# The end of a scan kernel: other planned costs, paired norms and other shares of engines behind the last scan

## The chip, the cores and the metric

The kernel runs on one core of a Trainium2 chip. The metric is the device time of one execution in microseconds (us), the median over runs. The engines are named as in the profile: PE is TensorE, PEld its weight loads, DVE is VectorE, ACT is ScalarE, POOL is GpSimd and SP the engine that here only issues transfers.

## The reference, cut to what matters

The input has 4 batches of 64 x 64 positions with 96 channels, in float32.

```
x = x + conv(group_norm(x))        # layer norm, projections, a scan over 4096 positions
t = x as [4, 4096, 96]
t = t + attn(layer_norm(t))        # linear attention: no softmax
t = t + ffn(layer_norm(t))         # 96 -> 384 -> 96, rounded to fp8 and fp16

# the scan, 96 channels x 16 states:
h = d * (A_t * h) + d * (B_t * u_t);  y = gate * sum(C_t * h)

# ffn, with q_mul to 5 exponent and 2 mantissa bits, q_acc to 5 and 10:
h = relu(q_acc(q_acc(q_mul(x) @ q_mul(W1)) + q_mul(b1)))
y = q_acc(q_acc(q_mul(h) @ q_mul(W2)) + q_mul(b2))
```

The attention has no softmax, so all keys and values of a batch shrink to one 97 x 96 matrix (called r here), and the attention of a position is a product with it. The matrix of a batch needs every position of the batch, so the attention and the feed-forward of a batch come only after its last scan.

## The kernel before, in words

A batch is cut into 8 chunks of 512 positions (`NCH`, `TC`), each held as 128 partitions x 4 rows (`J`) x 96 channels. There are 32 chunks. Each goes through 12 tiles of 128 partitions (32 channels x 4 states), so the scan stage has 384 steps (`K`). Each step does the projections on PE, the products and the scan on DVE, copies on ACT and a product on POOL. All other work is put beside these steps by a table of steps (`AT`, written by hand, through `at`): the preparation of chunks ahead (`front`), the `tail` of the chunk just scanned (state sum, gate, output projection, residual, layer norm, transposed copy, Gram matrix), `attn_matrix` once a batch, and the `ffn` of the batch before. The tile framework doesn't reorder: each engine works in the order in which the program writes its instructions.

What can't be put ahead of step 384 is left over: the last tail, the last `attn_matrix`, the feed-forward of all 8 chunks of the last batch, and parts of the feed-forward of the batch before (chunks 5, 6 and 7 of it). I write (b, i) for chunk i of batch b, counted from 0; the last batch is 3. This end is ordered by a planner (`Plan`, kept in `end`). `tail`, `attn_matrix` and `ffn` make jobs instead of table entries: an engine, a cost in us, the jobs it follows (`after`), buffers it takes and frees, and `late`, the time from the end of its instruction to the result being there. `run` schedules the jobs once by (time, rank, longest rest of the chain) and then 1500 times more with random offsets to the rank, keeps the order whose planned end is earliest, and writes the instructions in that order. The plan decides order alone; on the chip each engine waits for semaphores. Where PE is planned to be idle for over 0.8 us, `stay_awake` products are written to keep its clock up.

A layer norm (`LayerNorm`) has three steps: `stats` on DVE (`bn_stats`, `bn_aggr`), `rstd` on POOL (add eps, power -0.5, and for an apply on ACT also minus mean times root), then `apply` on ACT (four activations) or `apply_vector` on DVE (four tensor_scalar). The power works on 4 columns, one of each row of the partition.

One whole chunk in the end runs these steps: `fetch` (a transfer on SP), `attention` (PE), `residual` and `stats` (DVE), `rstd` (POOL), `apply` (ACT, or DVE where `vector` is true: chunks 0 and 4 of the last batch), `transpose` (PE), `quant_in` (ACT), three times `hidden` (PE), `round_hidden` (ACT) and `relu_vector` (DVE), then `quant` (ACT for i % 3 == 0, else POOL), `project_out` (PE), `round_out` (ACT), `bias_out` and `total` (POOL; on DVE for the last two chunks) and `store` (SP).

The lines of the profile named here: L836, L852, L845 the products and the scan of a step; L374 and L376 `stats`; L381, L395, L386 and L387 the four steps of `rstd`; L399 `apply`; L406 `apply_vector`; L900 `state_sum`; L979 `gram_sum`; L1044 to L1059 the chain to r; L1093 `fetch`; L1098 `attention`; L1103 `residual`; L1113 `transpose`; L1120 `quant_in`; L1124 `hidden`; L1141 `round_hidden`; L1145 `relu_vector`; L1150 and L1152 `quant` on ACT and POOL; L1158 `project_out`; L1165 `round_out`; L1170 `bias_out`; L1177 `total`; L1180 `store`; L1459 `stay_awake`; L620 the power of the group norm.

Of the kernel before, what the change touches and what calls it, by code (L numbers as in the profile page):

```python
# [17 lines left out]
P = 128  # L18
# [39 lines left out]
}  # L58
ON_POOL = (0, 2, 7, 8)
XBUFS = 15  # L60


@with_exitstack
def conv_attn_hybrid_kernel(
# [130 lines left out]
    mhalf = const.tile([P, J], F32, name="mhalf")  # L195
    nc.gpsimd.memset(mhalf, -0.5)

# [165 lines left out]

    class LayerNorm:


        def __init__(self, eps, nm):
            self.eps, self.nm, self.r = eps, nm, None

        def stats(self, src):  # L370
            st = small.tile([P, J, 6], F32, tag="st", name=f"st_{self.nm}")
            self.mv = small.tile([P, J, 2], F32, tag="mv", name=f"mv_{self.nm}")
            for j in range(J):
                nc.vector.bn_stats(st[:, j, :], src[:, j, :])  # L374
            for j in range(J):
                nc.vector.bn_aggr(self.mv[:, j, :], st[:, j, :])  # L376

        def rstd(self, shift=True):

            self.r = small.tile([P, J], F32, tag="rstd", name=f"rstd_{self.nm}")  # L380
            nc.gpsimd.tensor_scalar(self.r, self.mv[:, :, 1], self.eps, None, ALU.add)  # L381
            self.root()
            if not shift:
                return
            self.nmr = small.tile([P, J], F32, tag="nmr", name=f"nmr_{self.nm}")
            nc.gpsimd.tensor_scalar(self.nmr, self.mv[:, :, 0], -1.0, None, ALU.mult)  # L386
            nc.gpsimd.tensor_tensor(self.nmr, self.nmr, self.r, ALU.mult)  # L387

        def offset(self):

            self.r = small.tile([P, J], F32, tag="rstd", name=f"rstd_{self.nm}")
            nc.vector.tensor_scalar(self.r, self.mv[:, :, 1], self.eps, None, ALU.add)

        def root(self):
            nc.gpsimd.tensor_tensor(self.r, self.r, mhalf, ALU.pow)  # L395
# [19 lines left out]
    class Plan:  # L415
# [10 lines left out]
        def job(self, engine, cost, fn, *args, after=(), take=(), free=(), late=0.0):  # L426

            j = dict(
                engine=engine, cost=cost, fn=fn, args=args, take=take, free=free, late=late,
                after=[a for a in after if a], tail=None, end=None, rank=self.rank,  # L430
            )
            self.jobs.append(j)
            return j
# [5 lines left out]
        def run(self, fill=None):  # L439
# [17 lines left out]
            def schedule(bias, look):  # L457

                taken, back = {r: list(x) for r, x in self.taken.items()}, {}
                time, order = dict(self.time), []  # L460
# [3 lines left out]
                while ready:  # L464
                    best = None
                    for n in ready:
                        j = self.jobs[n]
                        t = max(time.get(j["engine"], 0.0), first[n])
                        for b in j["take"]:
                            r = b.split(":")[0]  # L470
                            if len(taken[r]) >= self.rings[r]:
                                x = taken[r][-self.rings[r]]
                                t = max(t, back[x] + self.HOP) if x in back else None
                            if t is None:
                                break
# [13 lines left out]
                    end = time[j["engine"]] = t + j["cost"]  # L489
                    for b in j["take"]:  # L490
                        taken[b.split(":")[0]].append(b)
# [44 lines left out]
    class GroupNorm:  # L536
# [82 lines left out]
        def root(self):  # L619
            nc.gpsimd.tensor_tensor(self.m[:, 1:2], self.v, mhalf[0:C, 0:1], ALU.pow)  # L620
# [60 lines left out]
    class Front:  # L681
# [3 lines left out]
        def __init__(self, b, i):  # L685
            self.b, self.i, self.nm = b, i, f"{b}_{i}"
            self.ln = LayerNorm(1e-3, f"c_{self.nm}")
            self.wd = {}
# [204 lines left out]
    def state_sum(g, last=None, first=None):  # L893
# [5 lines left out]
        for cg in range(NCG):  # L899
# [12 lines left out]
         "xs": 2, "xl": 2, "z": 2, "mv": 4},  # L912
# [16 lines left out]
    def tail(b, i):  # L929
# [68 lines left out]
        end.rank = 0  # L998
# [5 lines left out]
        if last:  # L1004
            for sh, late in ((0, 0.0), (2, 0.0), (3, 2.4)):
                w = job(f"wait{sh}", late, lambda: None)
                a = job("PE", 0.5, state_sum, g, sh, sh > 0, after=[a, w, end.last.get("o")],
                        take=["B:y"] if sh == 0 else [])
        else:
            assert state_sum in done  # L1010
        if ln.stats in done and ln.apply not in done:
            end.hold(f"mv:a{i}")
        if gated in done and project_out not in done:
            end.hold(f"yg:{i}")
        a = job("DVE", 0.7, gated, after=[a], take=[f"yg:{i}"], free=["B:y"])
        a = job("PE", 0.5, project_out, after=[a], take=[f"B:o{i}"], free=[f"yg:{i}"])
        end.last["o"] = a
        a = job("DVE", 0.56, residual, after=[a], free=[f"B:o{i}"])
        a = job("DVE", 1.1, ln.stats, t, after=[a], take=[f"mv:a{i}"])
        a = job("POOL", 1.3 if last else 1.8, ln.rstd, not last, after=[a])  # L1020
        if last:
            applied = job("DVE", 1.3, ln.apply_vector, xa, t, after=[a], free=[f"mv:a{i}"])
        else:
            applied = job("ACT", 1.55, ln.apply, xa, t, after=[a], free=[f"mv:a{i}"])
        if gram not in done:
            a = job("PE", 0.4, gram, after=[applied, end.last.get("gram")], take=[f"B:g{i}"])
            end.last["gram"] = job("DVE", 0.25, gram_sum, after=[a], free=[f"B:g{i}"])
        if transpose not in done:
            a = job("PE", 0.45, transpose, after=[applied], take=[f"C:a{i}"])
            a = job("ACT", 0.57, keep, after=[a], free=[f"C:a{i}"], take=[f"xat:{i}"])  # L1030
            end.last[b, i] = job("SP", 0.5, spill, after=[a], late=2.5, free=[f"xat:{i}"])
# [4 lines left out]
    def attn_matrix(b, s0):  # L1036
# [30 lines left out]
        end.rank, a = 0, end.last.get("gram")  # L1067
        for n, (args, out) in enumerate(chain):
# [4 lines left out]
            else:  # L1073
                a = end.job("PE", 0.3, mm, *args, after=[a], take=[f"B:r{n}"])
                a = end.last["r"] = end.job("DVE", 0.25, out, after=[a], free=[f"B:r{n}"])
# [5 lines left out]
    def ffn(b, i, s0):  # L1081
        nm = f"{b}_{i}"
        v, ln = {}, LayerNorm(1e-5, f"f_{nm}")
# [5 lines left out]
        vector = b == B - 1 and i % 4 == 0  # L1089
# [57 lines left out]
        def quant():  # L1147
            v["hq"] = sb("bu", [P, NK, TC], F8, f"hq_{nm}")
            if i % 3 == 0:
# [17 lines left out]
        def bias_out():  # L1167
            last_two = phase["end"] and b == B - 1 and i > NCH - 3
            v["yb"] = tile_of("yb", "xl", [P, J, C], F16, "yb")
            (nc.vector if last_two else nc.gpsimd).tensor_tensor(  # L1170
# [3 lines left out]
        def total():  # L1174
            v["o"] = tile_of("o", "z", [P, J, C], F32, "o")
            last_two = phase["end"] and b == B - 1 and i > NCH - 3
            (nc.vector if last_two else nc.gpsimd).tensor_tensor(v["o"], t, v["yb"], ALU.add)  # L1177
# [23 lines left out]
        end.rank = 1 + (b * NCH + i) // 4  # L1201
        if fetch in done and attention not in done:
            end.hold(f"xal:{nm}")
        if ln.stats in done and apply not in done:
            end.hold(f"mv:{nm}")
# [3 lines left out]
        def job(engine, cost, fn, *args, **kw):  # L1209
            return None if fn in done else end.job(engine, cost, fn, *args, **kw)  # L1210

        a = job("SP", 0.5, fetch, after=[end.last.get((b, i))], late=2.5, take=[f"xal:{nm}"])
        a = job("PE", 0.46, attention, after=[a, b == B - 1 and end.last["r"]], take=[f"A:a{nm}"],
                free=[f"xal:{nm}"])
        a = job("DVE", 0.57, residual, after=[a], free=[f"A:a{nm}"])
        a = job("DVE", 1.6, ln.stats, t, after=[a], take=[f"mv:{nm}"])
        a = job("POOL", 1.3 if vector else 1.8, ln.rstd, not vector, after=[a])
        a = job("DVE" if vector else "ACT", 1.9 if vector else 1.8, apply, after=[a], take=[f"xn8:{nm}"], free=[f"mv:{nm}"])
        a = job("PE", 0.45, transpose, after=[a], take=[f"C:{nm}"], free=[f"xn8:{nm}"])
        a = job("ACT", 0.6, quant_in, after=[a], take=[f"h:{nm}"], free=[f"C:{nm}"])  # L1220
        if hidden not in done:
            r, h, c = [], None, None
            for m in range(NK):
                h = job("PE", 0.24, hidden, m, after=[a, h], take=[f"M:{m}{nm}"],
                        free=[f"h:{nm}"] if m == 2 else [])
                c = job("ACT", 0.57, round_hidden, m, after=[h, c],
                        take=[f"rep:{nm}"] if m == 0 else [], free=[f"M:{m}{nm}"])
                r.append(job("DVE", 0.47, relu_vector, m, after=[c]))
            a = job(*(("ACT", 1.5) if i % 3 == 0 else ("POOL", 1.6)), quant, after=r, take=[f"bu:q{nm}"], free=[f"rep:{nm}"])
        a = job("PE", 0.5, project_out, after=[a], take=[f"A:y{nm}"], free=[f"bu:q{nm}"])  # L1230
        a = job("ACT", 0.48, round_out, after=[a],
                take=[f"xs:{nm}"], free=[f"A:y{nm}"])
        last_two = b == B - 1 and i > NCH - 3
        a = job(*(("DVE", 0.6) if last_two else ("POOL", 0.95)), bias_out, after=[a], take=[f"xl:{nm}"], free=[f"xs:{nm}"])
        a = job(*(("DVE", 0.8) if last_two else ("POOL", 0.92)), total, after=[a], take=[f"z:{nm}"], free=[f"xl:{nm}"])
        job("SP", 0.5, store, after=[a], late=2.5, free=[f"z:{nm}"])

# [159 lines left out]
    for b in range(B):  # L1397
        for i in range(NCH):
# [9 lines left out]
            first = min(24, AT["fetch"])  # L1408
# [43 lines left out]
    for s in sorted(steps):  # L1452
        if s >= K:
            call(s)
    awake = bank("D", [P, TC], "awake")
# [40 lines left out]
```

## Time and profile before

| | us |
|---|---|
| median of 3 runs | 1184.86 |
| lowest and highest run | 1181.39 and 1185.01 |
| span of the profiled execution | 1179.2 |
| the profiled execution's own time beside the span | not listed; the median stands 5.66 above the span |
| end of the last scan on DVE | 1104.26 |
| end of the last product with C on DVE | 1105.12 |
| the matrix r is copied | 1120.44 |
| end of the last total on DVE | 1173.23 |

The profile is one execution. Its page gives the busy time of each engine, 40 equal slices of the span, the chain that ended last and groups of instructions. A table of stretches gives busy times between two times, a timeline lists instructions with start and duration (neighbours of one kind merged), and the waits tell who waited for whom. The span up to about 1105 us is the scan stage, the last 74 us the end.

### The profile page before, as it was taken

Reading aid. Unit: us, or ns where it says so; the run is one execution under the profiler, and the core shown is the slowest. Engines: PE = TensorE matmul, PEld = TensorE weight load, DVE = VectorE, ACT = ScalarE, POOL = GpSimd, SP = SyncE. Lnnn points to the kernel's source line nnn. Section 1 sums busy time; section 2 is a strip of 40 time slices with the busy share of each in tenths; the row PEclk is TensorE's granted clock in tenths of the full one; section 3 lists DMA queues with packets and bytes.
Section 4 is the critical chain, followed back from the end, with each engine's and each line's share of the span. In section 5 each row is a group of like instructions: output and inputs, shape, how many; then the busy total and the mean of one; then the engine's idle time right before and its main releaser. Section 6 shows DMA issues by size and latency. Waiting matters only on the chain. (4 is left out here: it accounts for less than half of the span.)

```text
span 1179.2 us, 19184 instructions
## 1 busy us (share of the span) xinstructions
PE 1138.6 (97%) x5882; PEld 874.2 (74%) x5882; DVE 1113.3 (94%) x2079; ACT 812.9 (69%) x1833; POOL 1040.1 (88%) x1187
## 2 busy tenths in 40 slices
PE   6999999999999999999999999999999999999885
PEld 5777776777777777777777777777777777777563
DVE  6999999999999999999999999999999999999865
ACT  4666655655556777777777778777777777776475
POOL 5798888888889999999999999999999999988575
PEclk8999999999999999999999999999999999999987
DMA  7676776778876777778766776776777768766221
GB/s 184 141 165 145 169 153 156 161 163 178 177 161 148 154 162 166 163 164 191 162 160 151 170 174 159 173 165 156 156 159 159 174 155 182 159 134 146 67 65 51
DMA packets 104288, 182.12 MB, mean 154 GB/s; under 512 B 42637, under 2 KB 50769, under 8 KB 104186
## 3 DMA queue, kind: packets, MB, share of 16 engines
q1 hardware_dynamic: 90060, 106.96, 37.6%
q0 software_dynamic: 13536, 73.93, 31.4%
q8 instruction: 46, 0.75, 0.3%
q14 instruction: 56, 0.46, 0.1%
q10 hardware_dynamic: 590, 0.02, 0.0%
HBM read 69.12 MB, written 24.77 MB: 80 GB/s over the span
## 5 line engine op out<-in xcount | busy, mean ns | idle before, releaser
L836 POOL TENSOR_TENSOR bu<-bu,rep 128x512 f32<-128x512 f32 x384 | 511.9, 1343 | 42.7 <-ACT state L862 32.8
L852 DVE TENSOR_TENSOR_SCAN h<-Aps,state,bu 128x512 f32<-128x512 f32 x336 | 425.9, 1268 | 0.3 <-issue 0.2
L833 ACT ACTIVATE bu<-Bps,b_bac 128x512 f32<-128x512 f32 x384 | 262.8, 684 | 198.8 <-PE Bps L269 193.1
L845 DVE SCALAR_TENSOR_TENSOR Aps<-Aps,b_bac,rep 128x512 f32<-128x512 f32 x384 | 281.6, 733 | 4.7 <-PE Aps L269 4.3
L269 PE MATMUL Bps<-xs,w 128*128 128x512 f32 x768 | 267.1, 429 | 3.8 <-ACT bu L833 3.1
L269 PE MATMUL Aps<-xs,w 128*128 128x512 f32 x768 | 241.8, 396 | 1.2 <-DVE h L852 1.0
L885 POOL TENSOR_TENSOR ch<-ch,h 128x512 f32<-128x512 f32 x126 | 169.8, 1347 | 7.0 <-ACT ch L882 3.3
L269 PEld LDWEIGHTS Aps<-xs,w 128*128 128x128 f32 x768 | 143.9, 188 | 36.9 <-DVE h L852 2.7
L269 PEld LDWEIGHTS Bps<-xs,w 128*128 128x128 f32 x768 | 126.6, 190 | 45.8 <-ACT gx_ps L577 12.6
L269 PE MATMUL Aps<-xl,w 128*128 128x512 f32 x384 | 151.8, 395 | 0.0
L269 PE MATMUL Bps<-xl,w 128*128 128x512 f32 x384 | 151.5, 395 | 0.0
L269 PE MATMUL Dps<-xs,w 128*128 128x512 f32 x384 | 120.7, 395 | 0.0
L269 PE MATMUL Cps<-xs,w 128*128 128x512 f32 x384 | 120.6, 395 | 0.0
L876 DVE SCALAR_TENSOR_TENSOR ch<-Dps,b_bac,h 128x512 f32<-128x512 f32 x160 | 118.6, 741 | 0.4
L891 POOL DMA_DIRECT2D ch<-ch x94 | 88.9, 946 | 1.4 <-DMA ch<-ch 1.1
L269 PEld LDWEIGHTS Bps<-xl,w 128*128 128x128 f32 x384 | 72.3, 188 | 17.5
L269 PEld LDWEIGHTS Aps<-xl,w 128*128 128x128 f32 x384 | 72.1, 188 | 17.6
L269 PEld LDWEIGHTS Dps<-xs,w 128*128 128x128 f32 x384 | 72.1, 188 | 17.5
L269 PEld LDWEIGHTS Cps<-xs,w 128*128 128x128 f32 x384 | 72.1, 188 | 17.5
L882 ACT ACTIVATE ch<-Cps,b_bac 128x512 f32<-128x512 f32 x94 | 64.5, 686 | 24.2 <-PE Cps L269 24.2
L269 PE MATMUL Cps<-xl,w 128*128 128x512 f32 x192 | 75.8, 395 | 0.0
L269 PE MATMUL Dps<-xl,w 128*128 128x512 f32 x192 | 75.6, 394 | 0.0
(200 smaller groups left out, 2049.4 us busy)
## 6 DMA issues: line engine op xcount, KB each, us to landing
ch<-ch POOLq DMA_DIRECT2D x94, 768.0 KB, 6.7
rep<-ddd SPq DMA_DIRECT2D x124, 384.0 KB, 7.5
ddd<-dd SPq DMA_DIRECT2D x31, 384.0 KB, 3.2
xl<-lo SPq DMA_DIRECT2D x62, 128.0 KB, 2.4
x<-in_x_dram SPq DMA_DIRECT2D x32, 192.0 KB, 2.9
xatd<-xat SPq DMA_DIRECT2D x32, 192.0 KB, 3.6
xal<-xatd SPq DMA_DIRECT2D x32, 192.0 KB, 5.4
out_dram<-o SPq DMA_DIRECT2D x32, 192.0 KB, 2.5
```

Source lines behind the costliest of these rows:

```text
L269: nc.tensor.matmul(ps, lhsT=wt[:, n], rhs=mv, start=(n == 0), stop=(n == 2))
L833: nc.scalar.activation(self.bu, self.b_ps, AF.Identity, bias=self.bias(0))
L836: nc.gpsimd.tensor_tensor(self.bu, self.bu, rep[self.b, self.i][:, 1, self.cg], ALU.mult)
L845: nc.vector.scalar_tensor_tensor(self.a_ps, self.a_ps, self.bias(1), rep[self.b, self.i][:, 0, self.cg], ALU.add, ALU.mult,)
L852: nc.vector.tensor_tensor_scan(self.h, self.a_ps, self.bu, 0.0 if self.i == 0 else state[self.sh, self.cg], ALU.mult, ALU.add,)
L876: nc.vector.scalar_tensor_tensor(self.slot(), self.c_ps, self.bias(2), self.h, ALU.add, ALU.mult)
L882: nc.scalar.activation(self.ch, self.c_ps, AF.Identity, bias=self.bias(2))
L885: nc.gpsimd.tensor_tensor(self.ch, self.ch, self.h, ALU.mult)
L891: nc.gpsimd.dma_start(chs[g, 0], chs.pop((g, sh)), accum_op=ALU.add)
```

## The change

Seven things change. All but the second and third touch only the end.

1. The costs and `late` values of the end's jobs are other numbers: attention 0.87 for 0.46, statistics 0.91 for 1.1 or 1.6, relu 0.27 for 0.47, casts of ACT 0.48 for 0.57. The last shard of the last state sum is expected at 1.6 instead of 2.4.
2. `rstd` moves into a class `Roots`, which may hold the statistics of several norms and takes one power over all their columns. Adding eps and negating the mean become tensor_tensor with constant tiles instead of tensor_scalar. This form is used for every norm of the kernel that went through `rstd`, in the scan stage too.
3. In the last batch, chunks 1 and 2, 3 and 4, 5 and 6 share one `rstd` (`END_PAIR`); 0 and 7 stay single. The jobs of a chunk are split in `begin` (fetch to statistics) and `finish` (apply to store), with the shared `rstd` between.
4. A job can be marked `port`. The planner starts a marked job on DVE only after the last marked job on POOL has ended, and the other way round. Marked are `apply_vector`, `relu_vector`, `quant` on POOL, `bias_out` and `total`.
5. `apply` is on DVE for chunks 0, 2, 4, 6, 7 (`APPLY_DVE`), of the older batch too where the whole chunk is in the end; `quant` is on POOL for chunks 1 and 4 only, else on ACT; `bias_out` is on DVE for every whole chunk; `total` is on DVE for odd chunks.
6. Ranks: the last tail and the chain to r have -2, the older batch and the last transposes 0, a chunk of the last batch 1 plus the number of its pair. Before, the tails and the chain had 0, the older batch 6, the last batch 7 and 8.
7. The steps of `ffn` are created at step s + 18 instead of s + 21 (their own places in the table stay).

```diff
+MV_BUFS = {1: 4, 2: 2}
+END_RANKS = (-2, 0, 1)
+END_PAIR = (0, 1, 1, 2, 2, 3, 3, 4)
+APPLY_DVE = (0, 2, 4, 6, 7)
+QUANT_POOL = (1, 4)
+BIAS_DVE = (0, 1, 2, 3, 4, 5, 6, 7)
+TOTAL_DVE = (1, 3, 5, 7)
...
+    class Roots:
...
+        def root(self, shift=True):
+            if self.done:
+                return
+            self.done = True
+            n = len(self.of)
...
+                nc.gpsimd.tensor_tensor(
+                    self.r[:, k:m], self.mv[:, k:m, :, 1], eps_t[ln.eps][:, 0 : m - k], ALU.add
+                )
+            nc.gpsimd.tensor_tensor(self.r, self.r, mhalf[:, 0:n], ALU.pow)
+            if not shift:
+                return
+            nc.gpsimd.tensor_tensor(self.nmr, self.mv[:, :, :, 0], minus[:, 0:n], ALU.mult)
+            nc.gpsimd.tensor_tensor(self.nmr, self.nmr, self.r, ALU.mult)
...
         def rstd(self, shift=True):
-            self.r = small.tile([P, J], F32, tag="rstd", name=f"rstd_{self.nm}")
-            nc.gpsimd.tensor_scalar(self.r, self.mv[:, :, 1], self.eps, None, ALU.add)
-            self.root()
...
+            self.group.root(shift)
...
                         t = max(time.get(j["engine"], 0.0), first[n])
+                        if j["port"]:
+                            t = max(t, port.get("POOL" if j["engine"] == "DVE" else "DVE", 0.0))
...
-        end.rank = 0
+        end.rank = END_RANKS[0]
...
-            for sh, late in ((0, 0.0), (2, 0.0), (3, 2.4)):
+            for sh, late in ((0, 0.0), (2, 0.0), (3, 1.6)):
...
-        vector = b == B - 1 and i % 4 == 0
+        vector = whole and i in APPLY_DVE
...
-            if i % 3 == 0:
+            if i not in QUANT_POOL:
                 nc.scalar.activation(v["hq"], v["h16"], AF.Copy, saturate=False)
...
+        def begin(mv):
+            end.rank = END_RANKS[1] if b < B - 1 else END_RANKS[2] + END_PAIR[i]
...
+        def finish(a, mv):
...
+            e = "DVE" if whole and i in BIAS_DVE else "POOL"
+            a = job(e, 0.55 if e == "DVE" else 0.88, bias_out, e, after=[a], take=[f"xl:{nm}"], free=[f"xs:{nm}"], late=0.1, port=True)
+            e = "DVE" if whole and i in TOTAL_DVE else "POOL"
+            a = job(e, 0.5 if e == "DVE" else 0.88, total, e, after=[a], take=[f"z:{nm}"], free=[f"xl:{nm}"], late=0.1, port=True)
...
+        for key in sorted(groups):
+            group = groups[key]
+            mv = f"mv{len(group)}:end{key}"
+            stats = [begin([mv] if k == 0 else []) for k, (begin, _, _) in enumerate(group)]
+            a = end.job("POOL", 0.65 + 1.1 * len(group) ** 0.6, group[0][2].rstd, after=stats, late=0.1)
+            for k, (_, finish, _) in enumerate(group):
+                finish(a, [mv] if k == len(group) - 1 else [])
...
-            first = min(24, AT["fetch"])
+            first = min(18, AT["fetch"])
```

## The prediction

> **What bounds the kernel now.** I read the page's busy shares and slices first, then the table of stretches, then the timeline of each engine behind the last scan, then the waits and the chain that ended last.
>
> ```profile
> PE 1138.6 (97%) x5882; PEld 874.2 (74%) x5882; DVE 1113.3 (94%) x2079; ACT 812.9 (69%) x1833; POOL 1040.1 (88%) x1187
> ...
> PEclk8999999999999999999999999999999999999987
> ```
> ```profile
> 60.00:1100.00 1040.00, 1033.23 (x5269) 796.12 (x5268) 1014.61 (x1830) 733.23 (x1676) 954.38 (x1065) 1.00 0.73 161
> ```
> ```profile
> 1105.00:1121.00 16.00, 13.04 (x101) 9.38 (x96) 10.57 (x45) 7.90 (x18) 7.90 (x13) 1.00 0.22 62
> 1121.00:1173.30 52.30, 40.09 (x277) 28.58 (x276) 34.59 (x111) 37.49 (x76) 37.62 (x51) 0.83 0.21 58
> ```
>
> The columns of a stretch are its length, then the busy time of PE, PEld, DVE, ACT and POOL, then the granted clock. The scan stage (60 to 1100) is bound by TensorE and VectorE (1033 and 1015 of 1040 us). Behind the last scan no engine is the bound: in the last 52.3 us ACT is busy 37.5, POOL 37.6, DVE 34.6. So what is late there is order and blocking. This end is 68 us long and is all that the change can move by much. It has two parts.
>
> **Part one, to the matrix r** (the last c product ends at 1105.12, r is copied at 1120.44: 15.3 us). A chain of small steps.
>
> ```profile
> 1106.98 1.06 PE L900 MATMUL y_ps<-ch,fold 128*32 128x512 f32 x6
> ...
> 1111.85 0.90 POOL L381 TENSOR_SCALAR rstd_a<-mv_a 128x4 f32<-128x4 f32 x1
> ...
> 1113.83 1.46 POOL L1152 CAST hq<-h 128x1536 fp8e5<-128x1536 f16 x1
> 1113.90 2.17 DVE L406 TENSOR_SCALAR xa<-x,mv_a,rstd_a 128x96 f32<-128x96 f32 x4 [1.24 <-POOL rstd_a L395]
> ...
> 1120.18 0.26 DVE L1059 COPY rmat<-r_ps 97x96 f32<-97x96 f32 x1 [0.24 <-PE r_ps L1044]
> ```
>
> Columns: start, duration, engine, instruction. Three losses stand here. The last state sum starts 1.86 us after its input, because a transpose and an attention of other chunks were put ahead of it on PE. The POOL add takes 0.90 instead of its usual 0.23, beside VectorE's relus. The four applies take 2.17 beside a POOL cast.
>
> **Part two, eight chunks of feed-forward** (1120.44 to the last total at 1173.23: 52.8 us).
>
> ```profile
> L1145 DVE TENSOR_SCALAR h<-h,b_q x33: 318/345/1557, 1111.8 to 1168.1; 128x512 f16<-128x512 f16 x33
> ```
> ```profile
> L406 DVE TENSOR_SCALAR xn<-x,mv_f,rstd_f x8: 317/917/1484, 1147.6 to 1159.2; 128x96 fp8e5<-128x96 f32 x8
> ```
> ```profile
> L1177 DVE TENSOR_TENSOR o<-x,yb x2: 1150/1162/1174, 1165.1 to 1172.1; 128x384 f32<-128x384 f32 x2
> ```
> ```profile
> ACT h L1141 <- PE h_ps L1124: 6.9, 3, 3.1
> ```
> ```profile
> 1168.61 1.47 POOL hq L1152
> ...
> 1172.08 1.15 DVE o L1177
> ```
>
> The first three give min/median/max ns: the same relu takes 345 or 1557, the same apply 317 or 1484. Blocked time of DVE in part two: relus 13.9 us for 27, against 27 x 0.345 = 9.3, lost 4.6; applies 5.7 - 8 x 0.317 = 3.2; totals 2.3 - 2 x 0.5 = 1.3; together 9.1 us. So DVE's own work is 34.6 - 9.1 = 25.5. The wait says that ACT once stood 3.1 us for one hidden product, behind two attentions on PE at half clock. ACT is idle 14.8 us in all.
>
> **The Trainium skill.** "SBUF — State Buffer", Who interferes with whom: a VectorE operation in a 2-port mode, or with two SBUF inputs beside a GpSimd operation that reads SBUF, shares a port pair with GpSimd; the second to start blocks until the first is finished. The trace agrees for the casts and for yb and o: the final DVE total started beside a POOL o that ended at 1172.81 and ended 0.42 after it. It doesn't agree for the power: a relu of 0.35 ran at 1118.17, inside a power from 1118.16 to 1119.20. "TensorE: Matmul & The Clock Gate", Part 1: the array falls to half clock after an idle window and comes back after a busy one. The trace has 0.50 from 1123 to 1130.
>
> **The change, part by part.**
>
> *Norms in the scan stage.* Two tensor_scalar of 0.225 and 0.242 become tensor_tensor like the one beside them (0.20): -0.07 us on POOL, 96 times, some 6 us. POOL has 86 us of idle there and DVE and PE bind, so nothing is won; cost range -1 to +1. The new constants are three memsets of 0.1 in the first 9 us, before POOL's idle of 5.73: nothing. Power and statistics buffers keep four turns. Creating ffn's steps at +18 for +21 crosses no other creation (tails at +12 and +24), so nothing moves.
>
> *Ranks, costs and due times, part one.* The sum, the chain to r and the gram now go ahead (-2) of transposes and older chunks (0), and the last shard is expected at 1.6, not 2.4. Up to 1.75 of the 1.86 goes; late next is the gating on DVE. The exclusion, if the order keeps it, returns 0.67 on the add and 1.07 on the applies (2.17 - 1.1). Sum 3.5 at best, 0.5 at worst; I take 2.5.
>
> *Shares of engines, part two.* Counted from the timelines. POOL: 8 biases x 0.92 leave, net 3 totals x 0.95, 4 casts x 1.46, and pairing. A power on four columns takes 1.04, on one (the group norm's) 0.57, so 0.155 a column over 0.42; on eight I estimate 1.66 (bounds 1.04 and 2.08). Two norms of 1.94 become one of 2.45, three times: -4.3, and +0.4 for shifts that two norms now also compute. Sum -20, from 37.6 to about 17.6. ACT: three applies less (-4.5), four quantizations more (+5.8): 37.5 to 38.8. DVE: eight biases (0.56 each, measured), three totals (never seen alone; between 0.4 and 1.17, taken 0.56 like the residual of its size) and three applies at 1.1: +9.5, from 25.5 to 35.0, plus what stays blocked. POOL's streaming work falls from 25 to 7.5 us while DVE's share of the pair rises from 12.6 to 22, so the 9.1 scale to 9.1 x 0.30 x 1.75 = 4.8: DVE about 39.8. Beside an apply of the older batch (two, before r), DVE also takes 2.2 us that ACT's end did not wait for.
>
> So ACT and DVE stand near 39 each of now 52.8; neither can end before about 39 plus a head (first attention to first ACT step, about 6.5, of which older chunks fill 5) and a tail (product 0.7, round 0.5, bias and total 1.1). That is 43 at perfect overlap. ACT's idle was 14.8; I let it fall to 9.5, by 3 at the head (the stand for the hidden product) and 2.3 from applies and relus that are no longer blocked: 38.8 + 9.5 = 48.3, against 52.8, 4.5 us won (bounds +9 and -9).
>
> *Pairing's wait.* The first chunk of a pair waits for its partner's attention and statistics, about 1.5 us (residual and statistics take 1.52 in the timeline), three times. Its cover is the pair ahead, still in its hidden products. If that cover is gone, each wait is paid: 4.5 us, the size of the gain.
>
> *DMAs.* Spills, fetches and stores keep their number; only their order on SP moves. A store lies behind every total, so a late total also holds the fetches queued behind it; DMA is busy 0.21 here and no fetch ended a long wait of PE. *Fills* on PE follow planned gaps; larger PE costs leave fewer gaps and fewer fills, so the clock may drop lower than 0.83. An attention then takes 1.8 for 1.0. PE is not the bound; bounded at +2 us.
>
> Sum: 2.5 + 4.5 = **7.0 us**. Against the profiled span: 1179.2 - 7.0 = 1172.2. The page gives no further time of that execution; the median of the runs is 5.66 above the span, and I keep that distance: 1184.86 - 7.0 = **1177.9**.
>
> **Rivals.**
> *A, the forecast* (0.62): 1172 to 1182. *A+* (0.08): the order fits and both engines are above 85% busy in part two, 45 us; with 2.5 from part one about 1174.5, with the full 3.5 and shorter gaps down to 1169.
> *B, gain eaten by waits* (0.18): pairs wait for partners, PE colder. Part one's 2.5 less 1 to 2 us: 1183 to 1185. For it: DVE was idle 17.7 us in part two already, mostly waiting for ACT's h; a share moved to DVE doesn't shorten that. Also, nothing on the chip enforces the planned exclusion: the plan may simply not come true.
> *C, slower* (0.12): VectorE's in-order queue becomes the bound. It now holds residual, statistics, applies, relus, biases and half the totals; a bias waiting for ACT's y holds the relus behind it, and these hold ACT's quantization. Idle 17.7 and blocked 9.1 stay as they are, and 35.0 of work come on top: 61.8 us, +9.5, less 2.5: 1191.9. It decides from part two at 55.3 us on, when it eats part one too.
>
> **How the numbers follow.** A run tells about 0.3% (3.6 us) from no change. Faster: 0.62 x 0.95 + 0.08 + 0.18 x 0.1 = 0.69; same: 0.03 + 0.15 = 0.18; slower 0.13. The range reaches from 1170, with half of A+ left out, to 1188, with most of C left out.
>
> **What would show it.** Part one near 13 us, with the last state sum right behind the last c product; applies near 0.32 each; three powers on 8 columns near 1.7; POOL near 18 and ACT near 39 in part two, of some 48 us. The scan stage ending later or earlier than 1105 by over 1 us would make the account wrong, as would DVE idle staying at 17 with part two above 53.

## The result, and the profile after

The changed kernel takes 1171.01 us (median of 4 runs, 1169.27 to 1173.71), the kernel before 1184.93 (4 runs). The recorded ratio is 0.9905, with an interval of 0.9887 to 0.9924: 0.95% faster. The two medians alone lie 13.9 us apart (1.2%), and the runs of the kernel before reach from 1181.39 to 1185.47, so the size of the gain is known to some 2 or 3 us. The forecast was 1177.9, with 1170 to 1188 as its range; the measured median lies 1 us outside its main case (1172 to 1182). The span of the profiled execution fell from 1179.2 to 1167.5, by 11.7 us where 7.0 were forecast.

The page of after, in the lines that were shown of before:

```profile
PE 1129.6 (97%) x5868; PEld 865.4 (74%) x5868; DVE 1116.8 (96%) x2110; ACT 811.3 (69%) x1818; POOL 1008.9 (86%) x1166
...
PEclk7999999999999999999999999999999999999999
```

Stretches of after: the scan stage, then the end in two parts, cut at the same events as before (the end of the last product with C, the copy of r, the end of the last total on DVE). Columns as before: length, busy PE, PEld, DVE, ACT, POOL, granted clock.

```profile
60.00:1100.00 1040.00, 1033.83 (x5272) 795.76 (x5271) 1016.12 (x1831) 733.26 (x1676) 944.84 (x1066) 1.00 0.74 161
```
```profile
1104.83:1120.28 15.45, 13.85 (x112) 9.20 (x110) 11.66 (x53) 9.67 (x16) 6.74 (x13) 1.00 0.21 64
1120.28:1162.18 41.90, 28.92 (x250) 19.74 (x249) 36.04 (x133) 34.42 (x63) 18.09 (x27) 1.00 0.25 72
```

And before, cut at its own events:

```profile
1105.12:1120.44 15.32, 12.42 (x97) 8.88 (x91) 10.45 (x44) 7.34 (x16) 7.42 (x12) 1.00 0.23 65
1120.44:1173.23 52.79, 40.59 (x279) 29.08 (x279) 34.59 (x112) 38.05 (x77) 38.10 (x52) 0.83 0.21 57
```

The scan stage didn't move (its end lies at 1104.83 for 1105.12); POOL has 9.5 us less work in it, which nobody waited for. Part one, to the matrix r, won nothing: 15.45 for 15.32. Part two is 10.89 us shorter. What lies behind the last total is 5.32 for 5.97. The sum is 0.29 - 0.13 + 10.89 + 0.65 = 11.7.

Inside part two, ACT's idle time fell from 14.7 to 7.5 us (length less busy), and its busy time from 38.05 to 34.42. The durations of its instructions there sum to 43.3 us, for 44.7 before. So by this count 1.4 us of the fall is less work, although the new shares give ACT more of it: ACT did 2.3 us more before r (9.67 for 7.34). The other 2.2 us is overlap. An instruction that follows another without a gap starts before the record of the first ends, so a busy engine shows less than the sum of its durations:

```profile
1109.40 0.58 ACT L1202 CAST h<-h_ps 128x512 f16<-128x512 f32 x1 [1.64 <-PE h_ps L1185]
...
1135.04 2.02 ACT L1202 CAST h<-h_ps 128x512 f16<-128x512 f32 x4
```

One cast takes 0.58 us and four in a row take 2.02.

Two things that were late are nearly gone from the waits: ACT's stand for hidden products and VectorE's stand for ACT's casts. In part two of before they were (the line in the prediction has 6.9, because it counts part one too; the columns are the total, the number of waits and the longest):

```profile
DVE h L1145 <- ACT h L1141: 8.2, 5, 3.4
...
ACT h L1141 <- PE h_ps L1124: 3.9, 2, 3.1
```

The waits of ACT and of DVE's relu, after:

```profile
ACT xn L450 <- POOL nmr_f L413: 3.2, 1, 3.2
...
DVE h L1206 <- ACT h L1202: 1.3, 3, 0.6
...
ACT h L1202 <- PE h_ps L1185: 0.9, 2, 0.5
```

The instructions that were blocked before, min/median/max ns:

```profile
L1206 DVE TENSOR_SCALAR h<-h,b_q x33: 319/345/1614, 1111.1 to 1156.4; 128x512 f16<-128x512 f16 x33
```
```profile
L457 DVE TENSOR_SCALAR xn<-x,mv_f,rstd_f x28: 315/320/954, 1109.7 to 1147.4; 128x96 fp8e5<-128x96 f32 x28
```
```profile
L1236 DVE TENSOR_TENSOR o<-x,yb x5: 546/552/559, 1125.3 to 1161.6; 128x384 f32<-128x384 f32 x5
```

An apply now takes its free 320 ns in the median (917 before) and a total 552 (1162 before); relus are still caught, up to 1614.

### The profile page after: what moved, and what is told of

It reads as the page before. It is cut to its first block, busy times and chain, and to the rows that moved or that the text cites. A ratio compares the mean times of both kernels' runs of the same rounds, so it can differ in the third digit from the quotient of the medians.

```text
span 1167.5 us, 19144 instructions
## 1 busy us (share of the span) xinstructions
PE 1129.6 (97%) x5868; PEld 865.4 (74%) x5868; DVE 1116.8 (96%) x2110; ACT 811.3 (69%) x1818; POOL 1008.9 (86%) x1166
## 5 line engine op out<-in xcount | busy, mean ns | idle before, releaser
L283 PEld LDWEIGHTS Cps<-xs,w 128*128 128x128 f32 x384 | 72.0, 188 | 17.6
L283 PEld LDWEIGHTS Dps<-xs,w 128*128 128x128 f32 x384 | 72.0, 188 | 17.6
```

The lines of the kernel that those rows point to most:

```text
L283: nc.tensor.matmul(ps, lhsT=wt[:, n], rhs=mv, start=(n == 0), stop=(n == 2))
```

## The experiments

Theory P: the gain comes from the plan, that is from an order that fits the chip better (costs with their `late` values, ranks, exclusion). Theory S: it comes from the shares of engines, which take 20 us from GpSimd and with it VectorE's blocking; this was the prediction's account. Theory C: it comes from TensorE's granted clock, 0.83 before and 1.00 after in part two.

The table holds all kernels. The ratio is that to before as recorded with each run. Before had medians of 1182.17 us beside e1 to e4, 1184.19 beside e5 to e8 and 1181.35 beside e9 to e12, so across these groups ratios are compared and not medians. Parts one and two and the tail (the rest of the span behind the last total on DVE) are of the one profiled execution; runs of a kernel differ by some us, so small differences between their parts prove little.

"VectorE blocked" is an estimate for part two: for relus, applies, biases and totals on VectorE, the mean duration less the unblocked one (0.345, 0.317, 0.556 and 0.552 us), times their number. The prediction's 9.1 us for before is the same count from busy times; from the means it is 10.5.

| kernel | median us | ratio, interval | part one | part two | tail | ACT idle in part two | clock in part two | VectorE blocked |
|---|---|---|---|---|---|---|---|---|
| before | 1184.93 | 1 | 15.3 | 52.8 | 6.0 | 14.7 | 0.83 | 10.5 |
| after | 1171.01 | 0.9905 (0.9887 to 0.9924) | 15.5 | 41.9 | 5.3 | 7.5 | 1.00 | 4.6 |
| e1_plan | 1170.02 | 0.9892 (0.9874 to 0.9911) | 15.7 | 43.1 | 3.8 | 10.9 | 0.89 | 3.6 |
| e2_shares | 1179.40 | 0.9974 (0.9956 to 0.9991) | 15.2 | 52.0 | 5.3 | 13.3 | 0.86 | 3.7 |
| e3_single | 1166.55 | 0.9868 (0.9850 to 0.9886) | 15.6 | 41.2 | 3.1 | 6.8 | 0.90 | 2.9 |
| e4_no_port | 1170.55 | 0.9899 (0.9881 to 0.9917) | 15.3 | 43.6 | 3.0 | 8.6 | 0.92 | 4.1 |
| e5_before_fill | 1179.87 | 0.9962 (0.9947 to 0.9977) | 15.5 | 50.2 | 5.9 | 12.2 | 1.00 | 11.3 |
| e6_plan_old_ranks | 1176.87 | 0.9932 (0.9915 to 0.9948) | 17.0 | 47.2, to POOL's last total | 6.4 | 14.3 | 0.81 | 7.4 |
| e7_before_seed2 | 1179.04 | 0.9957 (0.9943 to 0.9972) | 15.2 | 50.2 | 5.4 | 12.5 | 0.88 | 11.0 |
| e8_before_new_ranks | 1177.83 | 0.9943 (0.9928 to 0.9957) | 15.4 | 52.3 | 3.0 | 16.5 | 0.76 | 8.7 |
| e9_last_total | 1169.39 | 0.9894 (0.9874 to 0.9914) | 15.5 | 41.9 | 3.1 | 7.3 | 0.96 | 4.0 |
| e10_single_fill | 1167.21 | 0.9880 (0.9862 to 0.9897) | 15.6 | 40.4 | 3.1 | 6.2 | 1.00 | 1.4 |
| e11_single_seed2 | 1168.32 | 0.9888 (0.9870 to 0.9905) | 16.8 | 42.3 | 3.1 | 7.5 | 0.82 | 1.2 |
| e12_after_seed2 | 1168.54 | 0.9889 (0.9869 to 0.9910) | 14.6 | 44.5 | 3.1 | 9.9 | 0.83 | 3.1 |

**e1_plan: the new plan alone.** From the kernel after, with old shares and no pairs:

```diff
-        vector = whole and i in APPLY_DVE
+        vector = b == B - 1 and i % 4 == 0
-            if i not in QUANT_POOL:
+            if i % 3 == 0:
-            e = "DVE" if whole and i in BIAS_DVE else "POOL"
+            e = "DVE" if b == B - 1 and i > NCH - 3 else "POOL"
-            groups.setdefault((b, END_PAIR[i] if b == B - 1 else i), []).append(w)
+            groups.setdefault((b, i), []).append(w)
```

(The total is changed like the bias, the quantization's job like its instruction, and the key of the norm like the groups. The new form of `rstd` and the earlier creation of `ffn`'s steps stay in, so they count with the plan here.)

> The new plan alone: measured costs, the GpSimd-VectorE exclusion and the new ranks, with the old shares of engines and every norm single. Before 1184.9, after 1171.0. If the plan (order) is the main source of the gain, over half of it stays: 1174 to 1178, and VectorE's blocked time in the last 8 chunks falls from 9 us to under 4 although GpSimd's work is still near 38. If the shares are the main source, GpSimd stays as loaded as before and blocks as before: 1181 to 1185. If TensorE's clock is the source, the time follows the granted clock behind r: under 0.9 there means no gain, near 1.0 means most of it.

Ratio 0.9892: all of the gain of after (0.9905, with overlapping intervals). The stretches of its profile:

```profile
1106.10:1121.82 15.72, 13.00 (x104) 7.46 (x104) 10.77 (x48) 11.30 (x23) 9.18 (x15) 0.97 0.24 70
1121.82:1164.93 43.11, 33.39 (x255) 25.07 (x252) 26.93 (x109) 32.17 (x68) 34.85 (x53) 0.89 0.26 71
```

GpSimd is busy 34.85 of 43.11 us here, more densely than before, and part two is 9.7 us shorter all the same. So GpSimd's load was not what held part two. ACT works 11.30 us before r, for 7.34 in before: the plan puts the older batch's work there.

VectorE is blocked less here too, some 3.6 us for 10.5, as the expectation had it for this case. Its relus and applies in part two of before, then of e1 (busy us, mean ns; idle time before them):

```profile
L1145 DVE TENSOR_SCALAR h<-h,b_q 128x512 f16<-128x512 f16 x27 | 13.9, 555 | 8.4 <-ACT h L1141 8.2
L406 DVE TENSOR_SCALAR xn<-x,mv_f,rstd_f 128x96 fp8e5<-128x96 f32 x8 | 5.7, 772 | 1.0 <-POOL rstd_f L395 1.0
```
```profile
L1206 DVE TENSOR_SCALAR h<-h,b_q 128x512 f16<-128x512 f16 x24 | 11.1, 488 | 9.5 <-ACT h L1202 9.5
L457 DVE TENSOR_SCALAR xn<-x,mv_f,rstd_f 128x96 fp8e5<-128x96 f32 x8 | 2.1, 327 | 0.0
```

So e1 alone doesn't tell order from blocking; e2 does. VectorE stands for ACT's casts as long as in before (9.5 us for 8.2), so that stand isn't what the plan saves here. On ACT, which has the same work to do in both kernels, the 9.7 us are 4.0 of work moved from part two to part one, 1.9 less busy time over both parts (43.47 us for 45.39: one cast runs before part one here, the rest is overlap) and 3.8 less idle.

**e2_shares: the new shares alone.** In the kernel before:

```diff
-        vector = b == B - 1 and i % 4 == 0
+        whole = s0 + max(AT["attention"], AT["residual_f"]) >= K
+        vector = whole and i in (0, 2, 4, 6, 7)
-            if i % 3 == 0:
+            if i not in (1, 4):
-            last_two = phase["end"] and b == B - 1 and i > NCH - 3
+            last_two = whole
```

(The last pair of lines is that of the bias; the total has `whole and i % 2 == 1`. The jobs of the plan follow suit, at the old costs.)

> The new shares alone (apply, quantization, bias and total on the new engines) in the kernel before, with its old costs, old ranks, no exclusion and single norms. If the plan is the main source: 1180 to 1188, VectorE in-order waits eat what GpSimd loses. If the shares are: 1174 to 1178. If the clock is: the time follows the granted clock behind r, 0.83 before.

```profile
1122.27:1174.28 52.01, 41.10 (x297) 30.14 (x294) 36.56 (x136) 38.73 (x67) 21.48 (x31) 0.86 0.21 58
```
```profile
L1146 DVE TENSOR_SCALAR h<-h,b_q 128x512 f16<-128x512 f16 x28 | 11.8, 434 | 5.5 <-ACT h L1142 4.7
...
L406 DVE TENSOR_SCALAR xn<-x,mv_f,rstd_f 128x96 fp8e5<-128x96 f32 x20 | 5.8, 354 | 0.6 <-POOL rstd_f L395 0.6
```

Ratio 0.9974: GpSimd's busy time in part two falls from 38.1 to 21.5 us and VectorE's blocked time from 10.5 to 3.7, and the time falls by a quarter of a percent. So in this order the prediction's mechanism (less load on GpSimd, less blocking of VectorE) works and hardly pays. The value is a rough one: its 15 runs reach from 1175.20 to 1186.40 us, wider than those of any other kernel here.

Before, e1, e2 and e3 below (the plan and the shares together, no pairs) form a square. The plan is worth 1.08% with the old shares (e1) and 1.06% with the new (e3 against e2); the shares are worth 0.26% with the old plan and 0.24% with the new, where the intervals of e1 and e3 overlap. This speaks for P and against S. All four are of the first seed of the search; e7, e11 and e12 below bear on that.

**e3_single: after without pairs.**

```diff
-            key = f"end{b}_{END_PAIR[i]}" if b == B - 1 else f"end{b}_{i}"
+            key = f"end{b}_{i}"
-            groups.setdefault((b, END_PAIR[i] if b == B - 1 else i), []).append(w)
+            groups.setdefault((b, i), []).append(w)
```

> The kernel after with every norm single (no shared power), the ranks of the chunks kept by pair. In after, ACT stood 3.2 us for the first pair's norm. If that wait is a cost of pairing and GpSimd, busy 18 of 42 us there, has room, single norms are as fast or faster: 1168 to 1171. If pairing pays (4.3 us of GpSimd work saved), they are slower: 1173 to 1176.

Ratio 0.9868, the lowest of all that ran. It seemed that pairing costs 4 us; e9, e11 and e12 below take most of that back.

**e4_no_port: after without the exclusion in the plan.**

```diff
-                        if j["port"]:
+                        if False:
                             t = max(t, port.get("POOL" if j["engine"] == "DVE" else "DVE", 0.0))
```

> The kernel after with the exclusion of GpSimd and VectorE left out of the planner's schedule; costs, shares and pairs as in after. If the exclusion does what its name says, blocked time of VectorE returns and the time rises by 2 to 4 us: 1173 to 1175. If the lower GpSimd load already removes the blocking, no difference: 1170 to 1172.

Ratio 0.9899, after 0.9905: no difference. The applies are blocked a little more (440 ns in the mean for 366), the relus less (405 for 459). With the new shares the exclusion does nothing that can be measured. With the old shares it wasn't left out by itself: whether it is what took VectorE's blocked time away in e1 is open.

**e5_before_fill: before, same order, more fills on PE.**

```diff
-                    for _ in range(int(max(0.0, t - self.time.get(e, t) - 0.4) / 0.4)):
+                    for _ in range(int(max(0.0, t - self.time.get(e, t) - (0.1 if phase["end"] else 0.4)) / (0.3 if phase["end"] else 0.4))):
```

> The kernel before, with the same order of work and more stay_awake products in TensorE's planned gaps of the end (from gaps of 0.4 us on, one for each 0.3 us, instead of gaps of 0.8, one for each 0.4). Before: clock 0.83 behind r, 0.50 to 0.54 in the first 10 us of it. If the clock is a main source of the gain: clock above 0.95 and 4 us or more faster, 1178 or less. If it is a side effect: the clock rises and the time stays within 2 us of before, 1181 to 1185, or gets longer where the fills delay products.

```profile
1120.42:1170.59 50.17, 40.00 (x309) 28.14 (x309) 35.37 (x112) 37.93 (x77) 38.14 (x52) 1.00 0.22 60
```

The clock is 1.00 and the ratio 0.9962. So the clock was worth about 4 us (1179.87 for 1184.19) to the kernel before, at no other change. But it isn't the cause of the gain as such: e1 has the whole gain at 0.89, e11 and e12 run at 0.82 and 0.83 and are as fast as after, and e8 gained at 0.76.

**e6 and e8: costs and ranks apart.** e6_plan_old_ranks is e1_plan with the old ranks; e8_before_new_ranks is before with the new ones.

```diff
 # e6
-END_RANKS = (-2, 0, 1)
+END_RANKS = (0, 0, 1)
-            end.rank = END_RANKS[1] if b < B - 1 else END_RANKS[2] + END_PAIR[i]
+            end.rank = 1 + (b * NCH + i) // 4
 # e8
-        end.rank = 1 + (b * NCH + i) // 4
+        end.rank = 0 if b < B - 1 else 1 + (0, 1, 1, 2, 2, 3, 3, 4)[i]
```

(e8 also gives the tails and the chain to r rank -2 and the last transposes 0.)

> The plan alone as in e1_plan (old shares, single norms), but with the old ranks: tails, the chain to r at 0, the older batch 6, the last batch 7 and 8. If the costs are what counts: as e1_plan, ratio 0.988 to 0.991. If the ranks are: most of the gain goes, ratio 0.996 to 1.0, and ACT works under 8 us before r instead of 11.3.

> The kernel before with the new ranks alone; old costs, shares and single norms. If the ranks are what counts: ratio 0.988 to 0.992 and ACT busy over 9 us before r. If the costs are: within 3 us of before, ratio 0.997 to 1.002.

0.9932 and 0.9943, each outside what either theory expected: each gives about half, and together (e1) 1.08% for 0.68 and 0.57. But another draw of the old plan gives 0.43% by itself (e7 below), with an interval that overlaps those of both, so how much of either half is owed to costs or ranks and how much to the draw isn't shown. With the new costs ACT works 11.67 us before r even at the old ranks; with the new ranks and old costs it works 8.85. Idle time of ACT in part two stays high in both (14.3 and 16.5) and falls only with the two together.

**e7_before_seed2: another order of the old plan.** `random.Random(2)` for `random.Random(1)` in the end.

> The kernel before with another seed of the planner's random search in the end, all else the same: how far the order that the search happens to find moves the time. If the old costs are wrong in a systematic way, the time stays within 3 us of before. If it was an unlucky order, it is 5 us or more faster with no other change.

0.9957: 5.1 us from nothing but another draw. The order that the kernel before happens to have is poorer on the chip than the one other draw that was tried. That is nearly half of the gain (0.43% of 0.95%). VectorE is blocked for 11.0 us in this order, as long as in before, and it is faster all the same.

**e9_last_total: the last GpSimd instruction.** In seven profiles (before, after, e1, e2, e5, e6, e7) the program ended 6.3 to 6.4 us after GpSimd's last instruction where that came late, and 3.0 to 3.1 us after the last total on DVE in the others.

```diff
-            (nc.vector if engine == "DVE" else nc.gpsimd).tensor_tensor(v["o"], t, v["yb"], ALU.add)
+            last = b == B - 1 and i == NCH - 2
+            (nc.vector if engine == "DVE" or last else nc.gpsimd).tensor_tensor(v["o"], t, v["yb"], ALU.add)
```

> The kernel after, in its order, with one instruction on another engine: the total of chunk 6, GpSimd's last instruction, goes to VectorE at the same place of the program. In six profiles the program ended 6.3 to 6.4 us after GpSimd's last instruction wherever that came late, and 3.0 to 3.1 us after VectorE's last total where GpSimd had ended long before. If GpSimd's end-of-program drain holds the end: 5.3 us behind the last total become 3.1, and the time falls by about 2 us against after (1169 for 1171). If those 2 us have another cause: no change, or 0.3 us longer for the longer VectorE queue.

The queue instructions of GpSimd behind the program's last line, of after and then of e9_last_total (min/median/max ns, first and last start):

```profile
L1587 POOLq DRAIN  x3: 34/93/6543, 1160.2 to 1167.3; - x3
```
```profile
L1588 POOLq DRAIN  x3: 34/93/6592, 1153.3 to 1165.1; - x3
```

GpSimd's queue has a drain of 6.5 us here (the longest of the three of each line). In after its record begins at 1160.2, with GpSimd's last total (1160.27, 0.91 us), and ends at 1166.8: 5.6 us behind the end of that total and 0.7 us ahead of the end of the program. In e9 it begins at 1153.3 and is over by 1159.9, before the last store is issued. Parts one and two are the same (15.45 and 41.86 for 15.45 and 41.90), the tail falls from 5.32 to 3.12 us. So 2.2 us of the profiled end hung on one total. The medians point the same way (0.9894 for 0.9905), but those intervals overlap.

**e10, e11, e12: fills for e3, and other draws for e3 and after.** e10_single_fill is e3_single with the fills of e5; e11 and e12 have seed 2 in the end.

> e3_single (the kernel after with single norms) in its order, with the denser stay_awake products of e5_before_fill: TensorE's clock behind r was 0.90 there. If the clock is worth time here as it was in the kernel before (4 us): 1163 to 1165. If ACT and VectorE, over 80% busy, bind: within 1 us of e3_single, 1166 to 1168.

> e3_single with another seed of the planner's search in the end. If its lead over after (4.4 us) is owed to the single norms: ratio to before under 0.988 again. If it was a lucky order: 0.989 to 0.993.

> The kernel after with another seed of the planner's search in the end. If the gain is owed to the costs, ranks and shares: ratio to before 0.988 to 0.993. If the order found with the first seed was luck: 0.994 to 0.998, where other seeds and ranks of the old plan lie.

e10: 1167.21, ratio 0.9880; no gain over e3 in the runs, though the clock went from 0.90 to 1.00. (In the profiles part two is 0.8 us shorter, and the scan stage, which is the same program, ended 1.8 us later.) e11 and e12, on one chip: 0.9888 and 0.9889. So with the second seed singles and pairs are equal. Of e3's lead over after (0.37%, some 4.4 us) the drain explains 2.2 us; the rest is then more likely a luckier order than the pairing, which one further draw of each can't prove. And after's gain over before doesn't hang on its own draw. Its size does hang on that of before: against e7, the old plan with the same second seed, e11 and e12 gain 0.7% (by the ratios of each to before).

## Why the prediction was right or wrong

The direction, the place (part two) and the range held. The account of where the time comes from did not, and two terms of the sum were off in opposite directions: part one won nothing for 2.5 us, and part two won 10.9 for 4.5. That the sum lies in the range is in part luck. By its time the result falls to case A+ (0.08), and not by what A+ says: part two is 41.9 us long for its 45, and below the 43 that the prediction took for the floor at perfect overlap.

*Part one, 2.5 us: failed, -0.1.* The three losses were read rightly, and two of them, GpSimd's add and the applies, went as worked out:

```profile
1107.02 1.06 PE L955 MATMUL y_ps<-ch,fold 128*32 128x512 f32 x6
```
```profile
1112.43 0.20 POOL L406 TENSOR_TENSOR rstd_a<-mv_a,eps 128x4 f32<-128x4 f32 x1 [3.43 <-DVE mv_a L435]
1112.71 1.51 POOL L409 TENSOR_TENSOR rstd_a<-rstd_a,mhalf 128x4 f32<-128x4 f32 x1
```
```profile
1114.26 1.05 DVE L457 TENSOR_SCALAR xa<-x,mv_a,rstd_a 128x96 f32<-128x96 f32 x4
1115.22 0.61 DVE L1206 TENSOR_SCALAR h<-h,b_q 128x512 f16<-128x512 f16 x2
1115.75 1.04 DVE L457 TENSOR_SCALAR xn<-x,mv_f,rstd_f 128x96 fp8e5<-128x96 f32 x4
1116.71 0.25 DVE L1034 TENSOR_TENSOR gram<-gram_ps,gram 97x97 f32<-97x97 f32 x1
```

The add takes 0.20 for 0.90 and the applies 1.05 for 2.17, as predicted. But the last state sum starts 2.19 us behind its input (1104.83), not right behind it: the rank of -2 is a preference within the search, and the order found has an attention and a transpose ahead of it as before. The power takes 1.51 for 1.04, and the Gram sum, whose product ended at 1115.77, stands 0.94 us behind two relus and an apply of the older batch on VectorE. The step assumed that a rank is obeyed.

*ACT's work in part two, 38.8: measured 34.4.* This is the term that broke the floor of 43. I counted ACT's part-two work as if the older batch stayed where it was. The plan moved 2.3 us of ACT's work ahead of r, into the idle time of part one. And I took ACT's busy time in a loosely filled stage for a fixed sum: in the fuller one the overlap of consecutive instructions grew by 2.2 us. The same idle time was in the stretch shown before (ACT 7.90 of 16), and I didn't ask who could fill it.

*ACT's idle time, 9.5: measured 7.5.* The size is near, the cause is not. I put it to applies and relus that are no longer blocked and to the head. VectorE is indeed blocked less (4.6 us for 10.5), but e2 has that too and wins only 0.26%; e1 has the old shares and GpSimd at 34.9 us, and wins; e4 has no exclusion, and wins. What goes in after, read from the waits, is standing in order, as at the hidden product of before. In e1 less of that goes (ACT idle 10.9 us), and more work stands ahead of r. That the plan gains in either way is shown; which of its parts does it is not.

*Counts that held:* GpSimd 17.6 forecast, 18.1 measured. Its power on eight columns, 1.66 forecast, took 1.64 once, but 1.96 and 2.04 the other two times. VectorE 39.8 forecast, 36.0 busy, with durations that overlap as on ACT (the busy times of its groups of instructions sum to 39.3); its blocked time is 3.1 for relus, 1.0 for applies and 0.5 for biases, 4.6 for the 4.8 forecast. Steady state at nothing: right.

*Pairing's wait:* its cover was gone once, at the first pair: ACT stood 3.2 us for the norm of chunks 1 and 2. Pairing isn't the only cause of such a stand: in e1, with single norms, ACT stood 6.4 us for its first norm behind r. As a whole, pairs and singles came out equal with the second seed (e11, e12).

*Rivals.* B (waits of pairs and a colder PE eat the gain) is refuted: the clock rose to 1.00, and one wait for a pair was paid. C (DVE's idle and blocked time stay, and its new work comes on top) too: DVE idles 5.9 us of 41.9, 18.2 of 52.8 before. The sentence under B that the exclusion may not come true was right (relus of up to 1614 ns), and it didn't matter.

*What I left out:* the drain, which was there to be read in before (5.97 us behind the last total, where the store's data moved for some 2). It holds the end of before and of after alike, so it cost the forecast little (0.65 us). And the clock, which I bounded as a cost: it rose to 1.00. To the old order that is worth 4 us (e5); to the new order no gain was seen (e10 against e3, and after at 1.00 against e12 at 0.83).

Which of the new costs matter most is open: they were tried only together, and in e1 and e6 together with the exclusion, the new form of `rstd` and the earlier steps of `ffn`.

## What to carry to other kernels

Where no engine is the bound of a stage, ask what order its instructions stand in before asking which engine is loaded: here moving 17 us off an engine was worth 0.25% (e2), and a new plan of the same work on the same engines 1.1% (e1). An order found by a random search is one draw: run a second seed of both versions before a difference of half a percent is given to the edit. And look at what lies behind the last useful instruction, per engine.

## What the runs showed of the hardware that was not expected

GpSimd's queue ends with a drain whose record begins with its last instruction and ends some 5.6 us behind the end of it (records of 6543, 6592 and 6858 ns in after, e9 and before, whose last instructions took 0.91, 0.95 and 1.22 us). Over the profiles where GpSimd's last instruction came late, the program ended 6.3 to 6.4 us after it; elsewhere 3.0 to 3.1 us after the last total on VectorE.

A relu on VectorE isn't blocked for the length of a power on GpSimd: in after, three relus took 0.86 us together inside a power on four columns, no more than three that follow each other unblocked (two took 0.61 at 1115.22, one takes 0.34). That power took 1.51 us for its usual 1.03; which work on VectorE stretched it isn't shown.

The time at which the scan stage ends fell into two groups over the executions of all these kernels, 1104.8 to 1105.5 and 1106.1 to 1107.3 us, with nothing changed in that stage but GpSimd's small operations, and nothing at all between before (1105.12) and e7 (1107.10). The cause was not looked for. A profiled span of these kernels therefore carries some 2 us that have nothing to do with their ends.
